# A re-ordered preamble, and the small loads moved from ScalarE's queue to SyncE's, in a fused cross-attention and rank-8 feed-forward kernel

## The chip, the cores and the metric

The kernel runs on one core of a Trainium2 chip. The metric is the device time of one execution in microseconds (us); lower is better. Five engines work side by side and meet only at semaphores: TensorE (PE in the profile: matmuls, with PEld for its weight loads), VectorE (DVE), ScalarE (ACT), GpSimd (POOL) and SyncE (SP), which computes nothing and here issues most DMA transfers. ScalarE can issue DMAs too ("ACTq" in the profile, "SPq" for SyncE's).

## The reference

All tensors are float32. x is (8, 1024, 1024): 8 batches of 1024 rows. A memory of 64 rows per batch is attended to, and then eight 1024 x 1024 matrices are applied to the same rows and summed.

```
h   = layernorm(x)
s   = h @ mem[b].T / sqrt(1024);  s = where(mask[b], s, -1e30)
x   = x + where(any(mask[b]), softmax(s) @ mem[b], 0)
h2  = layernorm(x)
x   = x + sum_r(h2 @ factors[r]) / sqrt(8) + bias        # r = 0..7
```

Because the eight products are only summed, `h2 @ factors[r]` summed over r is `h2 @ W` with W the sum of the eight matrices. The kernel forms W once, 32 MB of loads for 4 MB of weights.

## The kernel before, in words

**Tiling.** The 8192 rows are 16 groups of 512 (`g`); a group is four tiles of 128 rows (`t`), or two pairs of them (`q`). Two groups share a batch and so a memory.

**Program order is a table.** The kernel runs under a manual schedule: what a step issues to an engine stands in that engine's queue in the order of the text. `START` (L22) is a list of 259 steps that prepares the weights and the first two groups; `LOOP` then runs once per group. Every step is a small function; its arguments are numbers in the text. Each engine works through its own share of the steps strictly in that order and waits where an operand is not there yet.

**The ahead-of-loop work.** For groups 0 and 1: `load_rows g t` (L321) brings 128 rows; `row_stats g t` (VectorE, L371 and L372) takes mean and variance; `transpose_x_pe g h` (TensorE, L400, copied out by ScalarE at L401) transposes two tiles; `scores g` (L428) multiplies with the transposed memory, `scores_back g` turns it round, `softmax g` (VectorE L457 and L459, then ScalarE), `weights_back g`, `read_out g q n` (TensorE, L496) and `residual g q n` (VectorE, L504) add the attention's result to x. `norm_sums`, `norm_squares` and `normalize` are the second layernorm on ScalarE; `transpose_h_pe` transposes its result for group 0.

**The weights.** W is built in four shards `s` of 256 rows. `load_factor s r` (L704) brings a 1 MB piece of matrix r. A piece is then added in one of two ways: `add_factor s r` on VectorE, two adds of 128 x 1024 (L719; the first piece of a shard costs nothing, since its add comes with the second), or `sum_factor s r` on TensorE, four matmuls with the identity that sum into PSUM (L734). `add_sums s n` (L744) adds those PSUM sums to the weights, two VectorE adds. Shards 0 and 1 give the quarters b11 and t2 (at first b12), shards 2 and 3 give b21 and b22.

**The product.** It is a Strassen-Winograd scheme with seven products of halves instead of eight, so VectorE also forms differences of weights: t1 (L748), t2 (L750), t3 (L751) and t4 (L753). `product g q p` (L621) is one such product for a pair of tiles (128 x 512 by 512 x 512); `combine_rows` forms the sums of the rows (s1 to s4), `give g q p` (L634) adds a result to x. Products 2, 3, 4 and 5 are split once more by the same scheme into `part`, `combine_parts`, `combine_factors` (L764 to L767) and `give_part` (L685). A product that adds into the same PSUM bank as an earlier one waits until `give` has read the earlier value. `product 0 0 1` needs b11, `product 0 0 5` needs t1; `product 0 0 6` needs the finished t2, so all eight matrices of every shard.

**Buffers.** `bigs` are ten 8 KB-per-partition tiles that hold factor pieces, transposed rows, normalized rows and blocks in turn, given out first in, first out; `banks` are the eight PSUM banks, handled the same way.

**Later groups.** From group 2 on, rows are also loaded by `load_blocks g h` (L313, four DMAs of 256 KB) and transposed on VectorE by `transpose_blocks` (L385); from group 1 on, `relayout g q` (16 DMAs of 64 KB, L580) and `transpose_rows` (L589) transpose the normalized rows. `add_bias g q k` adds the bias on GpSimd (L570).

**Queues.** SyncE issues all loads and stores but these, which ScalarE issues: the mask to all partitions (L247) and twice to a small tile (L249), the memory of batch 0 (L271 and L272), and the bias (L264). Eight DMA completion semaphores (called lanes here) are shared by all DMAs, so a DMA waits until the one eight places before it has landed.

Of the kernel before, what the change touches and what calls it, by code (L numbers as in the profile page):

```python
# [30 lines left out]
add_factor 1 6; weights_back 0; scores_back 1; read_out 0 0 0; add_factor 0 2; read_out 0 1 0;  # L31
softmax 1; read_out 0 0 1; residual 0 0 0; residual 0 0 1; load_factor 1 2; load_factor 1 0;
load_factor 0 6; read_out 0 1 1; load_factor 1 5; weights_back 1; norm_sums 0 0; add_factor 1 3;
residual 0 1 1; load_factor 1 7; residual 0 1 0; add_factor 0 6; add_factor 1 7; sum_factor 1 0;
add_factor 1 2; load_factor 1 4; sum_factor 1 1; norm_squares 0 0; read_out 1 1 0;
load_factor 0 7; load_factor 0 3; read_out 1 0 1; load_factor 0 4; normalize 0 0 0;
normalize 0 0 1; norm_sums 0 1; sum_factor 1 4; residual 1 1 0; load_factor 3 7; add_factor 0 7;
transpose_h_pe 0 0 0; read_out 1 0 0; residual 1 0 0; norm_squares 0 1; load_factor 3 5;
read_out 1 1 1; residual 1 0 1; sum_factor 1 5; transpose_h_pe 0 0 1; load_factor 0 0;
residual 1 1 1; add_sums 1 1; load_factor 0 1; add_sums 1 0; add_factor 0 3; combine_rows 0 0 1;  # L40
sum_factor 3 5; add_factor 0 1; norm_sums 1 1; sum_factor 3 7; normalize 0 1 0; sum_factor 0 4;
normalize 0 1 1; add_factor 0 0; load_factor 3 3; load_factor 3 2; sum_factor 3 3; norm_sums 1 0;
combine_rows 0 0 2; add_sums 0 1; load_factor 3 4; norm_squares 1 0; load_factor 3 6;
add_factor 3 2; transpose_h_pe 0 1 0; add_sums 0 0; load_factor 3 0; load_factor 3 1;
add_factor 3 4; load_factor 2 3; load_factor 2 6; load_factor 2 1; add_factor 3 0;
add_factor 3 1; normalize 1 0 0; transpose_h_pe 0 1 1; load_bias; product 0 0 5; load_factor 2 2;
give 0 0 5; sum_factor 3 6; load_factor 2 7; add_bias 0 0 2; norm_squares 1 1; load_factor 2 4;
combine_rows 0 1 1; product 0 0 1; combine_rows 0 0 3; add_factor 2 6; product 0 1 1;
add_sums 3 1; combine_parts 0 4 1; add_sums 3 0; sum_factor 2 2; give 0 1 1; give 0 0 1;
# [5 lines left out]
part 0 4 1; combine_factors 4; product 0 0 7; give_part 0 4 1; combine_parts 0 4 4; part 0 4 5;  # L55
combine_rows 0 1 2; part 0 4 6; combine_rows 0 1 3; product 0 1 6; combine_factors 2;
give_part 0 4 6; combine_rows 0 1 4; combine_parts 0 2 1; part 0 2 1; give_part 0 4 5;
give 0 0 7; transpose_rows 1 0 0; add_bias 0 1 2; part 0 4 7; combine_parts 0 2 2;
load_blocks 2 0; part 0 4 3; transpose_blocks 2 1 0; give_part 0 4 3; transpose_rows 1 0 1;
part 0 2 5; combine_parts 0 2 3; give_part 0 2 5; give_part 0 4 7; add_bias 1 1 1; give 0 1 6;  # L60
combine_parts 0 3 1; give_part 0 2 1; product 1 0 1; transpose_blocks 2 1 1;
transpose_blocks 2 0 0; load_rows 2 2; transpose_blocks 2 0 1; load_rows 2 1; row_sums 2 0;
add_bias 0 1 1; part 0 3 1; part 0 4 4; give_part 0 3 1; normalize 1 1 1; transpose_blocks 2 1 2;
part 0 2 6; combine_parts 0 2 4; give_part 0 4 4; store 0 2; product 0 1 7; combine_rows 1 0 1;
part 0 2 3; transpose_blocks 2 0 2; load_rows 2 3; give 1 0 1; transpose_blocks 2 1 3;
row_sums 2 1; combine_parts 0 3 2; combine_parts 0 3 3; transpose_blocks 2 0 3;
combine_rows 1 0 2; row_squares 2 0; combine_factors 3; relayout 1 1; scores 2; product 1 0 6;
scores_back 2; give 0 1 7; combine_factors 5; give_part 0 2 6; part 0 3 6; part 0 2 2;
row_squares 2 1; softmax 2; give_part 0 3 6; combine_parts 0 3 4; part 0 3 5; give 0 1 5;
part 0 2 7; give_part 0 2 7; part 0 3 2; store 0 3; add_bias 0 0 1; give_part 0 3 5;  # L70
give_part 0 2 2; add_bias 0 1 0; add_bias 1 0 2; part 0 3 7;
"""

LOOP = """
# [32 lines left out]
def kernel(  # L107
# [17 lines left out]
    nc = tc.nc  # L125
    P = 128
# [53 lines left out]
    mask8 = const.tile([B, P // M, M], mask.dtype, name="mask8")  # L180
# [3 lines left out]
    bias_bc = const.tile([P, D], F32, name="bias_bc")  # L184
# [45 lines left out]
    st = {}  # L230
# [12 lines left out]
    def constants():  # L243

        room = bigs.take("mask", [P, 2, 8 * P], "mask_room")
        st["mask"] = room[:, 0, : B * M].bitcast(mask.dtype)[:, : B * M], room[:, 1, : B * M]
        nc.scalar.dma_start(st["mask"][0], mask.rearrange("b m -> (b m)").partition_broadcast(P))  # L247
        for h in range(P // M):
            nc.scalar.dma_start(mask8[:, h], mask)  # L249

    def masks():
        raw, maskf = st.pop("mask")
# [8 lines left out]
        banks.back("mask")  # L261

    def load_bias():
        nc.scalar.dma_start(bias_bc, bias.partition_broadcast(P))  # L264

    def load_memory(g: int):

        b = g // GPB
        m = work.tile([P, D], F32, tag="mem", name=f"mem_{b}")
        eng = nc.sync if g else nc.scalar  # L270
        eng.dma_start(m[:M], mem[b])  # L271
        eng.dma_start(m[M:], mem[b])  # L272
        st["mem", b] = m
# [550 lines left out]
```

## Time and profile before

| | us |
|---|---|
| median of 3 runs | 943.55 |
| lowest and highest run | 941.28 and 943.91 |
| the profiled execution | 941.54 |
| its span | 939.8 |
| TensorE busy | 916.9 (98% of the span) |
| VectorE busy | 783.4 (83%) |
| ScalarE busy | 458.9 (49%) |
| GpSimd busy | 265.2 (28%) |

Times below are counted from the start of the span. The clock granted to TensorE is 1.00 in every stretch. The DMA queues moved 167.04 MB; SyncE's queue carried 165.20 MB of it and ScalarE's 1.12 MB.

The DMA row of the profile shows how the work falls into two stages: in the first four of 40 slices (about 94 us) the queues move 313, 421, 420 and 421 GB/s, and afterwards less than half of that on average. The first stage is `START`: 32 factor pieces of 1 MB arrive, eight row tiles, one memory. From 107 us on TensorE stands still nowhere: all its idle time after that instant that the waits of TensorE name is zero. Matmul durations in the profile overlap (a 128 x 512 matmul is listed at 592 to 597 ns, while eight of them follow each other in 3.43 us, so 0.43 us each); sums below use the distance between starts.

### The profile page before, as it was taken

The page shows a single profiled execution, that of the slowest core. Times are in us where ns is not written, and L with a number is a line of the kernel's source. Part 1 is how long each engine was busy: PE and PEld are TensorE (multiplying, and loading weights), DVE is VectorE, ACT ScalarE, POOL GpSimd, SP SyncE. Part 2 cuts the span into 40 slices and gives each one's busy share as a digit, 9 for nine tenths or more (in the row PEclk, how much of TensorE's full clock was granted, in tenths as well). Part 3 has the DMA queues.
Part 4 walks back from the last instruction along what each step waited for, and adds up shares of the span by engine and source line. Part 5 has one row for each costly group of instructions (what it writes and reads, how often), then busy time and mean ns, then how long its engine had stood idle before and what let it go on. Part 6 is the DMA issues. An engine that isn't in the chain of part 4 may idle for free.

```text
span 939.8 us, 11731 instructions
## 1 busy us (share of the span) xinstructions
PE 916.9 (98%) x3637; PEld 578.2 (62%) x3637; DVE 783.4 (83%) x1619; ACT 458.9 (49%) x836; POOL 265.2 (28%) x355
## 2 busy tenths in 40 slices
PE   4899999999999999999999999999999999999998
PEld 4444456756657565666656575665756666665766
DVE  4799998969698896969698897969889797979876
ACT  4573233638464463737555373836545464745100
POOL 0202023515133231514233151513323151423221
PEclk9999999999999999999999999999999999999999
DMA  8999767476574847467484846558484856641412
GB/s 313 421 420 421 205 160 187 139 164 177 142 188 122 213 136 165 146 166 191 122 199 125 206 145 159 157 148 202 121 193 139 182 153 157 171 134 57 128 46 89
DMA packets 93565, 167.04 MB, mean 178 GB/s; under 512 B 12352, under 2 KB 71872, under 8 KB 89408
## 3 DMA queue, kind: packets, MB, share of 16 engines
q1 hardware_dynamic: 93024, 165.20, 61.9%
q10 hardware_dynamic: 480, 1.12, 0.4%
q8 instruction: 28, 0.46, 0.2%
q14 instruction: 33, 0.27, 0.1%
HBM read 101.25 MB, written 33.55 MB: 143 GB/s over the span
## 4 chain that ended last, share of the span: by engine, by line
PE 92%; DMA 6%; DVE 1%; ACT 1%; issue 0%; SPq 0%; POOL 0%; DVEq 0%
PE yu L621 34%; PE ro L496 6%; PE y5u L671 6%; PE y2u L671 6%; PE y4u L671 6%; PE y3u L671 6%; PE scT L428 6%; DMA f<-in_L_ffn_factors_dram 5%; PE y3v L671 3%; PE y5v L671 3%; PE y2v L671 3%; PE y4v L671 3%; PE sum L734 2%; PE y3z L671 1%; PE y2z L671 1%; PE y5z L671 1%
## 5 line engine op out<-in xcount | busy, mean ns | idle before, releaser
L570 POOL TENSOR_TENSOR x<-x,bias_bc 128x512 f32<-128x512 f32 x128 | 170.2, 1342 | 130.0 <-DVE x L685 51.6
L589 DVE STREAM_TRANSPOSE hT<-hb 128x1024 f32<-128x1024 f32 x60 | 72.7, 1231 | 59.7 <-DMA hb<-h 55.4
L532 ACT ACTIVATE junkz<-x 128x1024 bf16<-128x1024 f32 x64 | 67.6, 1057 | 109.0 <-DVE x L504 108.0
L621 PE MATMUL yu<-t,s 128*128 128x512 f32 x256 | 115.3, 593 | 1.9 <-DVE t L750 1.9
L621 PE MATMUL yu<-b,hT 128*128 128x512 f32 x256 | 114.9, 592 | 0.0
L621 PE MATMUL yu<-t,hT 128*128 128x512 f32 x256 | 112.6, 592 | 0.0
L563 ACT ACTIVATE h<-x,nb,rstd 128x512 f32<-128x512 f32 x128 | 96.5, 825 | 24.8 <-POOL rs L335 13.5
L504 DVE SCALAR_TENSOR_TENSOR x<-ro,rden,x 128x512 f32<-128x512 f32 x128 | 88.6, 746 | 13.2 <-PE ro L496 13.0
L634 DVE SCALAR_TENSOR_TENSOR x<-yu,x 128x512 f32<-128x512 f32 x128 | 82.8, 678 | 3.3 <-PE yu L621 3.2
L621 PEld LDWEIGHTS yu<-t,hT 128*128 128x128 f32 x256 | 48.6, 190 | 54.0 <-issue 52.6
L385 DVE STREAM_TRANSPOSE xT<-xb 128x256 f32<-128x256 f32 x224 | 81.6, 411 | 0.0
L621 PEld LDWEIGHTS yu<-t,s 128*128 128x128 f32 x256 | 48.5, 190 | 50.6 <-issue 46.3
L543 ACT ACTIVATE junky<-x,zm 128x1024 bf16<-128x1024 f32 x64 | 73.5, 1149 | 11.1 <-POOL zm L330 8.5
L621 PEld LDWEIGHTS yu<-b,hT 128*128 128x128 f32 x256 | 48.6, 190 | 48.4 <-issue 46.9
L330 POOL TENSOR_SCALAR zm<-zs 128x2 f32<-128x2 f32 x28 | 9.8, 351 | 223.9 <-ACT junkz L532 223.9
L347 ACT ACTIVATE junk<-x 128x1024 bf16<-128x1024 f32 x56 | 58.9, 1052 | 26.1 <-DMA x<-in_x_dram 25.2
L359 ACT ACTIVATE junk<-x,nmean 128x1024 bf16<-128x1024 f32 x56 | 64.3, 1148 | 7.1 <-POOL nmean L330 4.9
L496 PE MATMUL ro<-mem,eT 64*128 64x512 f32 x256 | 64.8, 615 | 0.6 <-DVE x L504 0.4
L428 PE MATMUL scT<-xT,memT 128*64 128x256 f32 x512 | 58.8, 382 | 0.0
L685 DVE SCALAR_TENSOR_TENSOR x<-y3u,x 128x256 f32<-128x256 f32 x64 | 26.7, 418 | 37.5 <-PE y3u L671 30.3
L428 PEld LDWEIGHTS scT<-xT,memT 128*64 128x64 f32 x512 | 35.3, 137 | 21.1 <-issue 4.3
L734 PE MATMUL sum<-f,ident 128*128 128x512 f32 x96 | 42.8, 597 | 2.3 <-DMA f<-in_L_ffn_factors_dram 2.1
(148 smaller groups left out, 1631.5 us busy)
## 6 DMA issues: line engine op xcount, KB each, us to landing
x<-in_x_dram SPq DMA_DIRECT2D x64, 512.0 KB, 3.5
f<-in_L_ffn_factors_dram SPq DMA_DIRECT2D x32, 1024.0 KB, 11.4
out_dram<-x SPq DMA_DIRECT2D x64, 512.0 KB, 3.1
hb<-h SPq DMA_DIRECT2D x480, 64.0 KB, 2.0
xb<-in_x_dram SPq DMA_DIRECT2D x112, 256.0 KB, 7.5
mem<-in_ctx_dram SPq DMA_DIRECT2D x14, 256.0 KB, 6.3
mem<-in_ctx_dram ACTq DMA_DIRECT2D x2, 256.0 KB, 9.4
bias_bc<-in_L_ffn_bias_dram ACTq DMA_DIRECT2D x1, 512.0 KB, 8.1
```

The lines of the kernel that those rows point to most:

```text
L385: nc.vector.transpose(xT[:, 2 * e + c].rearrange("p (t j) -> p t j", j=Q), xb.rearrange("p t (k e i c) -> p e c t k i", e=NC // 2, i=2, c= ...
L428: nc.tensor.matmul(ps[ts(h, M), : 2 * P], mT[:, c, :], st["xT", g, h][:, c, :], start=(c == 0), stop=(c == NC - 1),)
L496: nc.tensor.matmul(ps, eT[ts(h, M), q, :], m[ts(h, M), ts(n, H)], start=True, stop=True)
L504: nc.vector.scalar_tensor_tensor(xt, st.pop(("ro", g, q, n, h)), rden[:, k : k + 1], xt, ALU.mult, ALU.add)
L532: nc.scalar.activation(junk, st["x", g, 2 * h + q], AF.Copy, accum_out=s1[:, h : h + 1])
L543: nc.scalar.activation(junk, st["x", g, 2 * h + q], AF.Square, bias=nmean[:, h : h + 1], accum_out=ss[:, h : h + 1])
L563: nc.scalar.activation(to, fr, AF.Identity, bias=nb[:, h : h + 1], scale=rstd[:, h : h + 1])
L570: eng.tensor_add(xt, xt, bias_bc[:, ts(k % 2, H)])
L589: nc.vector.transpose(st["hT", g, q][:, h].rearrange("p c (t j) -> p t c j", j=Q), hb[:, h].rearrange("p t (c i) -> p t c i", i=Q),)
L621: nc.tensor.matmul(ps, lhs[:, c, :], wq[right][:, c, :], start=(first and c == 0), stop=(c == KH - 1), skip_group_check=True,)
L634: nc.vector.scalar_tensor_tensor(xt, st["y", g, q, key], ISR, xt, ALU.mult, ALU.add)
L671: nc.tensor.matmul(ps, lhs[:, c, :], right[:, c, :], start=(first and c == 0), stop=(c == 1), skip_group_check=True,)
```

## The change

It does three things.

1. `START` is replaced by another order of the same kinds of steps. It holds 259 steps as before. The rows of group 0 are loaded first, those of group 1 after factor pieces have been asked for; `scores 0` and `scores 1`, which were steps 23 and 32 (counted from 0), are steps 21 and 49. The factor pieces come in another order, shard by shard less strictly (pieces of shards 2 and 3 before the last ones of shard 1). Which pieces go to which engine changes too: `add_factor` 22 times instead of 20, `sum_factor` 10 times instead of 12.
2. The DMAs of the mask, of the memory of batch 0 and of the bias are issued by SyncE instead of ScalarE. `load_bias` was step 121 and is step 168, behind `relayout 1 0`; `scores 2`, step 235 before, is step 202.
3. Nothing in `LOOP` changes.

```diff
 START = """
-load_rows 1 0; constants; load_rows 0 0; load_rows 0 1; load_rows 0 2; load_memory 0;
-row_stats 1 0; load_rows 1 1; transpose_x_pe 0 0; row_stats 0 0; centre_memory 0; load_rows 0 3;
-transpose_x_pe 1 0; load_rows 1 2; masks; transpose_memory 0; load_factor 0 5; add_factor 0 5;
-row_stats 0 1; load_factor 1 6; transpose_x_pe 0 1; load_rows 1 3; row_stats 1 1; scores 0;
-scores_back 0; row_stats 0 2; load_factor 1 3; transpose_x_pe 1 1; row_stats 0 3;
-load_factor 0 2; softmax 0; load_factor 1 1; scores 1; row_stats 1 2; row_stats 1 3;
...
-sum_factor 2 7; load_factor 2 0; add_bias 0 0 3; add_factor 2 3; part 0 4 2; load_factor 2 5;
-combine_parts 0 4 2; add_factor 2 1; sum_factor 2 0; product 0 1 5; combine_rows 0 0 4;
-add_factor 2 4; give_part 0 4 2; combine_parts 0 4 3; load_memory 2; load_rows 2 0;
-normalize 1 0 1; relayout 1 0; add_factor 2 5; centre_memory 2; normalize 1 1 0; add_sums 2 1;
-product 0 0 6; load_blocks 2 1; add_sums 2 0; add_bias 0 1 3; give 0 0 6; transpose_memory 2;
...
+load_rows 0 0; load_rows 0 1; load_rows 0 2; constants; load_memory 0; load_rows 0 3;
+row_stats 0 0; centre_memory 0; load_rows 1 2; load_rows 1 3; row_stats 0 1; load_factor 1 5;
+load_factor 1 0; transpose_x_pe 0 0; masks; row_stats 0 2; transpose_memory 0;
+transpose_x_pe 0 1; row_stats 0 3; add_factor 1 5; load_factor 0 1; scores 0; load_rows 1 0;
+load_rows 1 1; row_stats 1 0; load_factor 0 0; add_factor 0 1; add_factor 1 0; scores_back 0;
+load_factor 0 5; softmax 0; load_factor 0 3; load_factor 0 7; transpose_x_pe 1 0;
+load_factor 0 4; load_factor 1 2; row_stats 1 1; row_stats 1 2; weights_back 0; add_factor 0 3;
+row_stats 1 3; transpose_x_pe 1 1; load_factor 0 6; load_factor 0 2; read_out 0 1 1;
+read_out 0 1 0; read_out 0 0 1; residual 0 1 0; read_out 0 0 0; scores 1; residual 0 0 0;
...
+load_factor 2 3; normalize 1 0 0; add_sums 3 1; combine_rows 0 0 2; add_sums 3 0;
+combine_rows 0 0 3; load_factor 2 5; sum_factor 2 1; normalize 1 1 0; sum_factor 2 7;
+add_factor 2 4; normalize 1 0 1; load_memory 2; product 0 1 5; give 0 1 1; sum_factor 2 5;
+add_factor 2 3; combine_rows 0 0 4; add_sums 2 1; add_sums 2 0; product 0 0 5;
+combine_parts 0 4 1; product 0 0 6; combine_factors 4; combine_rows 0 1 2; load_blocks 2 0;
+part 0 4 2; part 0 4 1; give 0 0 6; part 0 4 5; combine_parts 0 4 2; combine_rows 0 1 3;
+normalize 1 1 1; transpose_blocks 2 0 0; give_part 0 4 2; combine_parts 0 4 3; relayout 1 0;
+load_bias; combine_rows 0 1 4; centre_memory 2; transpose_memory 2; combine_parts 0 4 4;
+product 0 1 6; combine_parts 0 2 1; transpose_blocks 2 0 1; load_rows 2 2; give_part 0 4 1;
+part 0 2 1; load_blocks 2 1; product 0 0 7; part 0 4 6; give_part 0 4 5; combine_factors 2;
...
@@ constants
-        nc.scalar.dma_start(st["mask"][0], mask.rearrange("b m -> (b m)").partition_broadcast(P))
+        nc.sync.dma_start(st["mask"][0], mask.rearrange("b m -> (b m)").partition_broadcast(P))
         for h in range(P // M):
-            nc.scalar.dma_start(mask8[:, h], mask)
+            nc.sync.dma_start(mask8[:, h], mask)
@@ load_bias
-        nc.scalar.dma_start(bias_bc, bias.partition_broadcast(P))
+        nc.sync.dma_start(bias_bc, bias.partition_broadcast(P))
@@ load_memory
-        eng = nc.sync if g else nc.scalar
+        eng = nc.sync
```

More of the change, by code (lines that the diff above doesn't have):

```diff
@@ L31 @@
[L31 to L48, printed above, removed]
@@ L49 @@
-add_sums 3 1; combine_parts 0 4 1; add_sums 3 0; sum_factor 2 2; give 0 1 1; give 0 0 1;
-sum_factor 2 7; load_factor 2 0; add_bias 0 0 3; add_factor 2 3; part 0 4 2; load_factor 2 5;
-combine_parts 0 4 2; add_factor 2 1; sum_factor 2 0; product 0 1 5; combine_rows 0 0 4;
-add_factor 2 4; give_part 0 4 2; combine_parts 0 4 3; load_memory 2; load_rows 2 0;
-normalize 1 0 1; relayout 1 0; add_factor 2 5; centre_memory 2; normalize 1 1 0; add_sums 2 1;
-product 0 0 6; load_blocks 2 1; add_sums 2 0; add_bias 0 1 3; give 0 0 6; transpose_memory 2;
@@ L55 @@
[L55 to L71, printed above, removed]
+load_rows 0 0; load_rows 0 1; load_rows 0 2; constants; load_memory 0; load_rows 0 3;
@@ new lines @@
+row_stats 1 3; transpose_x_pe 1 1; load_factor 0 6; load_factor 0 2; read_out 0 1 1;
+read_out 0 1 0; read_out 0 0 1; residual 0 1 0; read_out 0 0 0; scores 1; residual 0 0 0;
+load_factor 3 2; residual 0 0 1; scores_back 1; add_factor 0 4; softmax 1; load_factor 3 6;
+load_factor 2 6; add_factor 0 6; residual 0 1 1; sum_factor 0 0; weights_back 1; norm_sums 0 0;
+load_factor 2 2; load_factor 1 6; read_out 1 0 1; norm_squares 0 0; add_factor 0 7;
+add_factor 1 2; load_factor 1 1; sum_factor 0 5; residual 1 0 1; load_factor 1 4; read_out 1 0 0;
@@ new lines @@
+add_factor 3 2; norm_sums 0 1; sum_factor 0 2; normalize 0 0 0; add_factor 3 6; add_sums 0 1;
+load_factor 2 0; add_factor 2 6; residual 1 0 0; load_factor 1 7; read_out 1 1 1;
+norm_squares 0 1; add_factor 2 2; add_sums 0 0; load_factor 3 4; sum_factor 1 6; norm_sums 1 0;
+normalize 0 0 1; add_factor 1 1; load_factor 1 3; residual 1 1 1; load_factor 3 7;
+read_out 1 1 0; normalize 0 1 0; residual 1 1 0; normalize 0 1 1; load_factor 3 1;
+add_factor 2 0; sum_factor 1 4; transpose_h_pe 0 0 0; add_factor 3 4; sum_factor 1 7;
@@ new lines @@
+load_factor 3 3; add_factor 1 3; add_sums 1 1; add_sums 1 0; add_factor 3 1;
+transpose_h_pe 0 1 0; transpose_h_pe 0 1 1; load_factor 3 0; load_factor 3 5;
+transpose_h_pe 0 0 1; add_factor 3 3; product 0 1 1; add_factor 3 0; norm_squares 1 0;
+load_factor 2 1; combine_rows 0 0 1; add_factor 3 7; combine_rows 0 1 1; product 0 0 1;
+sum_factor 3 5; norm_sums 1 1; load_factor 2 7; load_factor 2 4; give 0 0 1; norm_squares 1 1;
+load_factor 2 3; normalize 1 0 0; add_sums 3 1; combine_rows 0 0 2; add_sums 3 0;
@@ new lines @@
+load_bias; combine_rows 0 1 4; centre_memory 2; transpose_memory 2; combine_parts 0 4 4;
+product 0 1 6; combine_parts 0 2 1; transpose_blocks 2 0 1; load_rows 2 2; give_part 0 4 1;
+part 0 2 1; load_blocks 2 1; product 0 0 7; part 0 4 6; give_part 0 4 5; combine_factors 2;
+give 0 0 5; give_part 0 4 6; part 0 4 3; transpose_blocks 2 1 0; transpose_blocks 2 1 1;
+transpose_blocks 2 0 2; give_part 0 2 1; part 0 2 5; transpose_blocks 2 0 3;
+transpose_blocks 2 1 2; transpose_blocks 2 1 3; give_part 0 4 3; part 0 4 7; add_bias 0 0 2;
@@ new lines @@
+combine_parts 0 2 2; add_bias 0 0 3; give_part 0 4 7; load_rows 2 0; scores 2; add_bias 0 1 2;
+part 0 2 6; add_bias 0 0 1; transpose_rows 1 0 0; give 0 1 5; add_bias 0 1 1; give 0 0 7;
+part 0 4 4; transpose_rows 1 0 1; give_part 0 2 5; give_part 0 2 6; combine_parts 0 2 3;
+combine_parts 0 2 4; give 0 1 6; give_part 0 4 4; combine_parts 0 3 1; part 0 3 1;
+combine_rows 1 0 1; combine_parts 0 3 2; load_rows 2 1; store 0 2; load_rows 2 3; product 1 0 1;
+part 0 2 2; row_sums 2 0; give 1 0 1; part 0 2 3; part 0 2 7; give_part 0 3 1; row_squares 2 0;
@@ L72 @@
+combine_parts 0 3 3; combine_factors 3; combine_rows 1 0 2; combine_factors 5; product 0 1 7;
+part 0 3 5; scores_back 2; part 0 3 6; give_part 0 3 6; relayout 1 1; row_sums 2 1;
+product 1 0 6; row_squares 2 1; part 0 3 7; combine_parts 0 3 4; give 0 1 7; add_bias 1 0 2;
+softmax 2; give_part 0 2 7; give_part 0 3 5; give_part 0 2 2; add_bias 0 1 3; store 0 3;
+add_bias 0 1 0; add_bias 1 1 1; part 0 3 2;
 """
```

## The prediction

> **What bounds the kernel now.** I read the busy shares first, then the waits of TensorE over the whole span, then the order of time of TensorE and VectorE up to 130 us. TensorE is busy 98% of the span; its named waits come to 18 us, and all lie ahead of 107.5 us:
>
> ```profile
> PE tp L400 <- DMA x<-in_x_dram: 11.1, 2, 7.9
> PE sum L734 <- DMA f<-in_L_ffn_factors_dram: 2.1, 3, 1.0
> PE yu L621 <- DVE t L750: 1.9, 1, 1.9
> ```
>
> So the time is the instant at which `product 0 0 6` starts, plus TensorE's work behind it, plus what TensorE waits behind it (nothing now). That instant is set by this chain, TensorE first, then VectorE:
>
> ```profile
> 101.99 3.60 PE L621 MATMUL yv<-t,s 128*128 128x512 f32 x8
> 107.47 3.70 PE L621 MATMUL yu<-t,s 128*128 128x512 f32 x8 [1.89 <-DVE t L750]
> ...
> 102.40 2.36 DVE L719 TENSOR_TENSOR b<-b,f 128x1024 f32<-128x1024 f32 x2 [1.03 <-DMA f<-in_L_ffn_factors_dram]
> 104.87 1.29 DVE L744 TENSOR_TENSOR b<-sum,b 128x512 f32<-128x512 f32 x2
> 106.19 1.22 DVE L750 TENSOR_TENSOR t<-b,t 128x1024 f32<-128x1024 f32 x1
> ```
>
> The last factor piece lands at 102.4, VectorE adds it, adds the PSUM sums and forms t2, and TensorE starts at 107.47. The stage is limited by three things at once, as the windows show (columns: stretch, its length, busy us and instructions of TensorE, its loads, VectorE, ScalarE, GpSimd; clock; DMA share; GB/s):
>
> ```profile
> 20.00:45.00 25.00, 23.15 (x135) 12.97 (x135) 19.62 (x35) 14.41 (x39) 5.12 (x7) 1.00 1.01 420
> 45.00:70.00 25.00, 23.33 (x71) 10.46 (x67) 23.25 (x27) 18.77 (x33) 1.08 (x3) 1.00 1.01 420
> 70.00:95.00 25.00, 24.46 (x69) 11.46 (x68) 24.22 (x28) 8.68 (x15) 6.50 (x8) 1.00 1.01 421
> ```
>
> DMA is full, TensorE 93 to 98% busy, VectorE 78, 93 and 97%. A change gains only if it relieves all three.
>
> **Part 1: the loads.** TensorE waits for its seventh factor piece until 37.29 and VectorE for its 23rd until 77.00: 39.71 / 16 = 2.48 us a piece. The queues never starve, so in the new order the k-th piece (with all eight row tiles ahead of it) lands at 37.29 + 2.48 (k - 7) - g, g being what the start gains. What is g? The first 12 us move little: 208 GB/s on average up to 10 us against 420 later. SyncE's fourth load waits there 4.6 us for the mask, its first factor 2.8 us for the memory, since the eight lanes are shared:
>
> ```profile
> SPq L321 <- DMA mask_room<-in_mask_BxS_bk_dram: 4.6, 1, 4.6
> SPq L704 <- DMA mem<-in_ctx_dram: 2.8, 1, 2.8
> ```
>
> The upper end is g = 3: some 1.5 us lost between 8 and 12 us at 209 to 270 GB/s, and as much ahead of 6 us. The Trainium skill (DMA: Bandwidth & Descriptors, "Issuing engines are not separate DMA queues") speaks against a gain: DMAs of different engines run on the same 16 DMA engines and interleave, and a second issuing engine saves only issue time. By it g = 0, and SyncE pays ScalarE's issues (0.41 + 0.88 + 0.63 + 0.71 = 2.6 us), which is hidden, since its next load waits for the first to land anyway. The nearest row takes the rule's side in part: memory landed 9.4 us after issue on ScalarE's queue at the start, and 8.6 us on SyncE's at 95 us. It is slow by itself. But the mask no longer stands in the lanes ahead of the row tiles, and the bias (0.5 MB, 1.2 us) no longer ahead of the last pieces. I take g = 1. The last (32nd) piece then lands at 37.29 + 62.0 - 1 = 98.3, 4.1 us earlier than now; its four identity matmuls (1.7) end at 100.0. TensorE's early start is worth nothing: with rows 0 0 and 0 1 first it begins near 6 us instead of 11.6, but `transpose_x_pe 1 0` then waits for tiles that lie behind three factor pieces. `scores 1` ends near 40 us instead of 31. TensorE catches up later, for it has two `sum_factor` fewer: 8 x 0.43 = 3.4 us, and these are off the path, because VectorE is what comes last.
>
> **Part 2: VectorE up to t2.** Its queue is in order, and `row_stats 1 0` now stands ahead of every add. Tile 1 0 lands one tile (1.25) and one piece ahead of the fourth piece: 37.29 - 3 x 2.48 - 1 - 2.48 - 1.25 = 25.1 us. Until then VectorE idles some 10 us. From there to the end of t2 it has, by distances between starts in the trace:
>
> - 4 `row_stats` x 1.40 = 5.6 (two of these were done by 23 us before)
> - 18 pairs of adds x 2.27 = 40.9 (before 16; two more cost 4.5)
> - 8 `residual` x 1.31 = 10.5; 7 pairs of `add_sums` x 1.27 = 8.9
> - 6 weight differences = 7.3; 5 `combine_rows` x 0.61 = 3.1; 2 gives = 1.2; softmax 1.4
>
> Together 78.8. The same list for before gives 75.0 where the trace has 76.2 (84.5 us from 22.96 to 107.45 less 8.3 idle), so I add 1.7%: 80.1. One wait goes in: the pair that needs the sixth piece (33.8) is reached at 32.4, 1.4 us. Later pieces are there: the 22nd lands at 73.5 and is needed at 73.6. t2 is ready at 25.1 + 80.1 + 1.5 = **106.7**, 0.8 earlier than now, though loading ended 4 us earlier. In this list the differences t2 and t4 are priced quiet; one t2 difference took 1.89 us before while GpSimd added the bias (85.0 to 86.3), 1.22 otherwise. The bias adds now all come later, where they may cost as much: five of them at up to 0.67 each, 0 to 3.4 us, mostly beside slack; I take 0.
>
> **Part 3: behind `product 0 0 6`.** TensorE's work there grows by `part 0 4 2`, which was ahead of it: 0.86. Then VectorE's queue against TensorE's, both counted from 106.7: VectorE forms t3, t4, `combine_factors 4` and s2 by 7.3, TensorE reaches t4 0.3 too early and s2 another 0.4 too early. `scores 2` now comes 18 us behind `product 0 0 6` (before 27.7). Its chunks wait for `transpose_blocks 2 1`, which VectorE reaches at 17.0 and ends at 21.5; TensorE stands 0.5. Sum of waits 1.2. Afterwards TensorE is behind VectorE again: `part 0 2 6` at 22.6 needs s2 at 22.2, `product 1 0 1` at 25.2 needs rows transposed at 23.7.
>
> SyncE in this stretch: `relayout 1 0` waits for the buffer of `add_factor 2 4` (100.7), issues 16 DMAs at 0.64 (their distance from 108.7 on) to 0.91 (the mean of 97.92 to 112.51), then bias 0.36, rows 0.45 and four blocks at 0.5, and the blocks land 7.2 later: 121 to 125. Needed at 106.7 + 17.0 = 123.7. I take 121, as the slow issues before were those beside the last factor. GpSimd waits for the bias but nothing on TensorE's path waits for it soon.
>
> **Sum:** -0.8 + 0.86 + 1.2 = +1.3 us on the profiled execution's 941.54 (span 939.8): 942.8. That execution is 2.0 below the median of three (943.55); I place the forecast half way between the two bases, 943.8, rounded to **944**. About 0.3% (2.8 us) is what a measurement of this kernel can tell from no change.
>
> **Rivals.**
> 1. *Loading sets it, faster.* If VectorE's tile comes with g = 3 (23.1) and the ledger needs no 1.7%, t2 would follow loading: 96.3 + 1.7 + 3.4 (`product 0 0 5`) = 101.4 at best, and VectorE at 103.4. Product 0 0 6 is then 4.1 early: 941.5 - 4.1 + 0.9 + 0.7 = 939.0. For it: the first 12 us are visibly slow. Against: two adds more on an engine that was 97% busy, and slow memory loads.
> 2. *The blocks land late, slower.* `load_blocks 2 1` stands behind 16 relayout DMAs and the bias, and `scores 2` was moved forward. It decides once they land after 123.7. At 0.91 an issue they are issued by 118, and as slow as before (two sets of blocks took 114 to 124 us) they land at 128: 4.3 us of VectorE in order and so of TensorE: 942.8 + 4.3 = 947.1, 948 on the half-way basis. For it: the order of SyncE's queue. Against: in the quiet stretch issues were 0.64 apart.
> 3. *Nothing.* The stage is bound by three resources, and the two adds just fill what the loads gain: that is nearly the main case.
>
> **Chances.** Main case 0.55, own range 940.5 to 948.5; rival 1 0.22, 939 to 940; rival 2 0.23, 947 to 951. From these: faster by over 0.3% (below 940.7) 0.21, slower by over 0.3% (above 946.4) 0.39 (all but 0.03 of rival 2, and 0.19 of the main case, because such a ledger leaves waits out more easily than in), within 0.40. Range 939.5 to 949.5.
>
> **What would show it.** In the profile after: last factor piece landing near 98 (wait of TensorE or VectorE for f); VectorE idle from about 14 to 25 us waiting for x; TensorE waiting several us for VectorE ahead of `product 0 0 1` (b11) and again ahead of `product 0 0 6`, which starts near 106.7; short waits behind it at L671 and L428. A start of `product 0 0 6` near 103 speaks for rival 1, a wait of `transpose_blocks` on xb near 124 for rival 2. The forecast is wrong if row tile 1 0 lands far from 25, or if LOOP's first group shows waits on TensorE.

## The result and the profile after

The changed kernel takes 944.68 us (median of 11 runs, 943.72 to 947.61), the kernel before 941.54 (median of 11 runs beside them, 941.0 to 945.68). The ratio is 1.0029, with a 95% interval of 1.0015 to 1.0043: slower by 0.3%. The profiled execution of the changed kernel took 944.41 us (span 942.6), that of before 941.54 (span 939.8): 2.9 us apart.

These are TensorE's longest waits in the changed kernel (us in total, times, longest). All lie ahead of `product 0 0 6`:

```profile
PE tp L401 <- DMA x<-in_x_dram: 7.8, 4, 4.2
PE tp L401 <- DVE t L745: 2.8, 1, 2.8
PE sum L735 <- DMA f<-in_L_ffn_factors_dram: 2.4, 3, 1.4
PE memTp L302 <- ACT memc L287: 2.4, 1, 2.4
```

The row of before that had VectorE's t2 as the last releaser (`PE yu L621 <- DVE t L750: 1.9`) has no counterpart. TensorE no longer waits for t2. The order of time of TensorE shows what it did instead (start, length, line, tiles, count; in brackets an idle time ahead of it and its releaser):

```profile
77.35 1.49 PE L401 MATMUL tp<-ident,h 128*128 128x128 f32 x8 [2.78 <-DVE t L745]
78.63 8.59 PE L622 MATMUL yu<-b,hT 128*128 128x512 f32 x16
87.06 10.46 PE L735 MATMUL sum<-f,ident 128*128 128x512 f32 x24
97.36 3.60 PE L622 MATMUL yv<-t,s 128*128 128x512 f32 x8
101.56 3.70 PE L735 MATMUL sum<-f,ident 128*128 128x512 f32 x8 [0.61 <-DMA f<-in_L_ffn_factors_dram]
105.10 3.60 PE L622 MATMUL yv<-t,s 128*128 128x512 f32 x8
108.54 3.60 PE L622 MATMUL yu<-t,s 128*128 128x512 f32 x8
```

From 77.35 on it works with one gap of 0.61 us. The row at 108.54 is `product 0 0 6`. Count backwards from it: one product, one sum, one product, three sums. Each of them is four matmuls, which stand in the trace as eight records (x8), 0.43 us apart. That makes six blocks of 3.43 us (the distance of the last two starts), 20.6 us behind 87.06, and the gap at the last piece. VectorE over the same time:

```profile
24.09 1.29 DVE L372 BATCH_NORM_STATS2 stx<-x 128x6 f32<-128x512 f32 x2 [9.77 <-DMA x<-in_x_dram]
...
104.26 0.68 DVE L745 TENSOR_TENSOR b<-sum,b 128x512 f32<-128x512 f32 x1
105.30 0.69 DVE L745 TENSOR_TENSOR b<-sum,b 128x512 f32<-128x512 f32 x1 [0.36 <-PE sum L735]
106.03 1.22 DVE L751 TENSOR_TENSOR t<-b,t 128x1024 f32<-128x1024 f32 x1
```

t2 is ready at 107.25 (106.03 + 1.22), and TensorE comes for it only 1.29 us later. The three long windows (columns as in the prediction):

```profile
20.00:45.00 25.00, 19.96 (x103) 12.84 (x100) 18.21 (x30) 8.44 (x27) 1.21 (x2) 0.80 1.01 419
45.00:70.00 25.00, 22.45 (x62) 8.95 (x61) 24.88 (x30) 19.83 (x36) 3.56 (x6) 1.00 1.01 421
70.00:95.00 25.00, 22.22 (x66) 11.08 (x65) 23.73 (x26) 16.55 (x27) 5.62 (x6) 0.93 1.01 421
```

DMA is as full as before. TensorE is busy 80 to 90% instead of 93 to 98%, and its granted clock, 1.00 all through before, is 0.80 and 0.93. Windows of 5 us show where:

```profile
25.00:30.00 5.00, 3.94 (x16) 3.25 (x16) 4.83 (x10) 1.46 (x8) 0.00 (x0) 0.50 1.01 421
30.00:35.00 5.00, 4.75 (x23) 4.03 (x25) 3.47 (x6) 4.54 (x11) 0.00 (x0) 0.62 1.01 418
...
75.00:80.00 5.00, 2.65 (x10) 1.76 (x11) 4.86 (x7) 2.06 (x4) 0.00 (x0) 0.82 1.01 421
80.00:85.00 5.00, 5.00 (x11) 2.09 (x10) 5.00 (x6) 4.84 (x10) 2.81 (x3) 0.84 1.02 423
```

**Where the 2.9 us come from.** `product 0 0 6` starts 1.07 us later (108.54 against 107.47). Behind it TensorE has `part 0 4 2` more (0.86), its starts fall behind by 0.61 more up to 152 us and by 0.27 more in the loop (both are differences of starts; its waits name no cause for them): TensorE's last y3v group starts at 936.89 instead of 934.08, 2.81 us later.

The 1.07 us are a balance of larger sums. Up to `product 0 0 6`, TensorE of before is busy 89.29 us of 107.47, TensorE of after 88.55 of 108.54. The changed kernel has two sums and `part 0 4 2` less in that stretch, 2 x 3.43 + 0.86 = 7.7 us. But it is busy only 0.74 us less, so the rest of its work took some 7.0 us longer. The lowered clock accounts for about that: (1 - clock) x 5 us, summed over the windows below 1.00 (0.86, 0.50, 0.62, 0.82, 0.84), is 6.8 us. And it is not busy for 20.0 us instead of 18.2. So -7.7 + 7.0 + 1.8 = +1.1. This account says what TensorE's time consisted of, not which wait ended last; that is what the runs below are for.

### The profile page after: what moved, and what is told of

Same layout as the page of the kernel before. It is cut to its first block, busy times and chain, and to the rows that moved or that the text cites. A ratio compares the mean times of both kernels' runs of the same rounds, so it can differ in the third digit from the quotient of the medians.

```text
span 942.6 us, 11708 instructions
## 1 busy us (share of the span) xinstructions
PE 917.8 (97%) x3621; PEld 579.5 (61%) x3621; DVE 787.3 (84%) x1623; ACT 459.4 (49%) x836; POOL 267.6 (28%) x355
## 4 chain that ended last, share of the span: by engine, by line
PE 88%; DMA 7%; DVE 3%; SPq 1%; issue 0%; ACT 0%; DVEq 0%; ACTq 0%
PE yu L622 33%; PE ro L497 6%; PE y5u L672 6%; PE y2u L672 6%; PE y3u L672 6%; PE y4u L672 5%; PE scT L429 5%; DMA f<-in_L_ffn_factors_dram 3%; PE y3v L672 3%; PE y5v L672 3%; PE y2v L672 3%; PE y4v L672 3%; DMA xb<-in_x_dram 2%; PE sum L735 2%; PE y3z L672 1%; PE y2z L672 1%
## 5 line engine op out<-in xcount | busy, mean ns | idle before, releaser
L438 ACT ACTIVATE scTs<-scT,maskT 128x256 f32<-128x256 f32 x16 | 7.6, 473 | 93.9 <-PE scT L429 93.9
```

## The experiments

Theories: **A**, the new order makes the loss, and the queue does not; **B**, the queue makes part of it. **C**, TensorE comes last ahead of `product 0 0 6`; **D**, VectorE does, as the prediction had it. The runs were timed beside the kernel before, whose median was 941.57, 941.53 or 941.46 us (23, 11 and 27 executions). A ratio is to that kernel, with its 95% interval.

### The order alone, the queue alone

The two parts of the change, one each:

```diff
 START = (the new order)
-        nc.sync.dma_start(bias_bc, bias.partition_broadcast(P))
+        nc.scalar.dma_start(bias_bc, bias.partition_broadcast(P))
```

(likewise mask and memory of batch 0), and

```diff
-START = (the new order)
+START = (the order of before)
         nc.sync.dma_start(bias_bc, bias.partition_broadcast(P))
```

> The new order with mask, memory and bias on ScalarE's queue as before. Theory A (the order makes the loss: two adds more on VectorE, b11 finished later, so TensorE starts its products late): 944 to 946 us, ratio to before 1.002 to 1.004. Theory B (the queue makes the loss, by putting slow small loads ahead of the row tiles): 941 to 942.5, ratio within 0.001 of 1.

> The old order with mask, memory and bias on SyncE's queue. Theory A: 940.5 to 942 us, ratio 0.999 to 1.0005; row tiles at the start land up to 3 us earlier, but factor pieces only about 0.7 us earlier. Theory B: 944 us or more, ratio 1.002 or more.

Measured: the order alone 945.12 us (944.31 to 946.12), ratio 1.0033 [1.0022, 1.0044]. The queue alone 942.57 (940.60 to 951.82, 14 runs), ratio 1.0020 [1.0001, 1.0039]. The order alone brings the whole loss: A. The queue alone gains nothing that the time shows; its median lies between the two forecasts, and its interval, 0.01 to 0.39%, leaves room for a small loss too. In its profiled execution (941.42 us) `product 0 0 6` starts 0.86 us earlier than before, and the time is no different; but six of its 14 executions lie above 944 us, of before 3 of 23. In the order-alone run, TensorE's order of time has the last piece later than in the changed kernel:

```profile
97.66 3.60 PE L622 MATMUL yv<-t,s 128*128 128x512 f32 x8
102.69 3.70 PE L735 MATMUL sum<-f,ident 128*128 128x512 f32 x8 [1.43 <-DMA f<-in_L_ffn_factors_dram]
106.23 3.60 PE L622 MATMUL yv<-t,s 128*128 128x512 f32 x8
109.66 3.60 PE L622 MATMUL yu<-t,s 128*128 128x512 f32 x8
```

So under the new order the move to SyncE's queue goes with 1.1 us at `product 0 0 6` in the profiled executions; the medians, 0.44 us apart, do not tell the two kernels apart.

### One sum more, one sum less

A factor piece moved from VectorE to TensorE, and another from TensorE to VectorE, each from the changed kernel:

```diff
-add_factor 3 0
+sum_factor 3 0
```

```diff
-sum_factor 2 7
+add_factor 2 7
```

> The changed kernel with add_factor 3 0 turned into sum_factor 3 0: one pair of adds (2.27 us) less on VectorE, one sum (eight matmul records, 3.44 us) more on TensorE, late in the stage. Theory C (as measured: TensorE works without a gap from 78 us to product 0 0 6 and is last): about 3.4 us slower than the changed kernel, 947.5 to 948.5. Theory D (as predicted: VectorE is last and TensorE has 3.5 us of slack there): 1 to 2 us faster than the changed kernel, 942.5 to 943.5.

> The changed kernel with one factor piece of quarter 2 (piece 2 7) moved the other way than in the one-more-sum run: sum_factor to add_factor, 3.43 us less on TensorE, some 2.3 us more on VectorE. By the prediction's own picture (VectorE comes last ahead of product 0 0 6) t2 is 2.3 us later and so is the time, about 947. By theory C (TensorE comes last, and VectorE was 1.3 us ahead of it: t2 ready at 107.25, product 0 0 6 at 108.54) the first 1.3 us cost nothing and VectorE takes over as the last: product 0 0 6 near 109.5 (+1.0), the time +0.5 to +1.2 on the changed kernel, 945.2 to 945.9. So the split is balanced within a piece, and no choice of it brings the loss back.

One sum more: 947.10 us, ratio 1.0057 [1.0042, 1.0072], 2.4 us above the changed kernel. From 83.53 on TensorE runs without a gap, and it starts `product 0 0 6` at 111.10:

```profile
83.53 3.70 PE L735 MATMUL sum<-f,ident 128*128 128x512 f32 x8 [0.65 <-DMA f<-in_L_ffn_factors_dram]
87.06 3.60 PE L622 MATMUL yu<-b,hT 128*128 128x512 f32 x8
90.50 10.46 PE L735 MATMUL sum<-f,ident 128*128 128x512 f32 x24
...
111.10 3.17 PE L622 MATMUL yu<-t,s 128*128 128x512 f32 x7
```

The added sum is the row at 83.53. VectorE lost a pair of adds and still the start moved 2.56 us later: C, and D falls. It is 2.56 and not 3.43 because the 0.88 us that the changed kernel loses at the last piece are gone (and so the time, forecast as 947.5 or more, is 947.10).

One sum less: 945.85 us, ratio 1.0043 [1.0031, 1.0055]. `product 0 0 6` starts at 109.11, as forecast, and now it does wait for t2:

```profile
109.11 3.70 PE L622 MATMUL yu<-t,s 128*128 128x512 f32 x8 [0.67 <-DVE t L751]
```

Each engine is the last one as soon as it is given one piece more. The split of the changed kernel is balanced to within one piece, and neither of these two neighbours is better.

### The quarter that TensorE waits for, earlier

Pieces 1 7 and 1 3 are loaded ahead of 2 0 and 3 4, and added ahead of them, so that shard 1 is complete sooner and TensorE does not wait at 77 us (the cut shows the adding):

```diff
-add_factor 2 0; sum_factor 1 4; transpose_h_pe 0 0 0; add_factor 3 4; sum_factor 1 7;
-load_factor 3 3; add_factor 1 3; add_sums 1 1; add_sums 1 0; add_factor 3 1;
+add_factor 1 3; sum_factor 1 4; transpose_h_pe 0 0 0; sum_factor 1 7;
+load_factor 3 3; add_sums 1 1; add_sums 1 0; add_factor 2 0; add_factor 3 4; add_factor 3 1;
```

> The changed kernel with the pieces of shard 1 loaded and added ahead of pieces 2 0 and 3 4, so that b11 is complete some 4 us earlier; same steps, same counts. Theory C1 (what holds product 0 0 6 is the late b11 and the slow clock behind TensorE's wait there): products with b11 start near 74 instead of 78.6 at clock 1.00 (eight matmul records in 3.43 instead of 4.2 us), product 0 0 6 starts 1 us or more earlier, 943.5 or less. Theory C2 (the last factor piece, landing at 101.6, and TensorE's 6.9 us behind it hold it just as well): same earlier products, but product 0 0 6 near 108.4 and the time within 0.5 us of 944.7.

Measured: 945.32 us (944.73 to 946.29), ratio 1.0037 [1.0024, 1.0051]. TensorE's order of time:

```profile
75.01 7.03 PE L622 MATMUL yu<-b,hT 128*128 128x512 f32 x16
86.98 12.82 PE L735 MATMUL sum<-f,ident 128*128 128x512 f32 x24 [4.93 <-DMA f<-in_L_ffn_factors_dram]
99.63 3.60 PE L622 MATMUL yv<-t,s 128*128 128x512 f32 x8
```

The wait at 77 us is gone, the two products start 3.6 us earlier and run at full clock. Nothing comes of it: TensorE then waits 4.93 us for the 27th factor piece, starts its sums within 0.1 us of the time in the changed kernel, and runs them 2.4 us longer, at a clock of 0.50 just behind the wait. The idle time had only moved, as the second theory said; that the slow clock would move with it was not foreseen, and `product 0 0 6` starts at 109.93 instead of the 108.4 of that theory.

### The memory later, and the waiting filled

The memory load, which stands right behind the last factor piece in SyncE's queue, moved behind the first blocks; in the second run also the 16 transposes ahead of the wait at 77 us issued twice into the same place:

```diff
-add_factor 2 4; normalize 1 0 1; load_memory 2; product 0 1 5
+add_factor 2 4; normalize 1 0 1; product 0 1 5
...
-combine_rows 0 1 2; load_blocks 2 0;
+combine_rows 0 1 2; load_blocks 2 0; load_memory 2;
```

```diff
+                    for _ in range(twice):
-                    nc.tensor.transpose(ps[:, ts(c * n + t, P)], cols, ident)
+                        nc.tensor.transpose(ps[:, ts(c * n + t, P)], cols, ident)
```

> The changed kernel with load_memory 2 moved behind load_blocks 2 0, so that no 64-row memory load follows straight on the last factor piece in Sync's queue. Theory E1 (the memory load shares the DMA engines with the last piece and stretches its tail from some 98 to 101.5 us): the last piece lands by 99.5, the 0.61 us in which TensorE waits for it are gone, product 0 0 6 starts near 107.9 instead of 108.5, and the time is some 0.6 us below the changed kernel's 944.7. Rival E2 (the tail has another cause: the pieces' own period): the last piece still lands at 101 to 101.7, TensorE still waits 0.5 us or more, and the time is that of the changed kernel, 944.2 to 945.2.

> The run with the memory load later, and besides the 16 transposes of h for the second quarter, which end 2.8 us before TensorE gets its next bank, are each issued twice into the same place (same result), so that about 1.9 of these 2.8 us are filled with work that adds nothing. Theory K1 (the waiting just before lowers the granted clock in 75 to 85 us, and that costs the two b11 products 8.4 - 6.9 = 1.5 us): the clock there goes from 0.82/0.84 to above 0.93, the products take 7.0 to 7.4 us, product 0 0 6 starts about 1 us earlier than in the run with the memory load later alone, and the time is about 1 us lower. Rival K2 (the clock follows something that lies further back, such as the 20 to 35 us stretch, or the waiting only moves): the clock in 75 to 85 stays below 0.88 and the products at 8 us or more, or TensorE waits the gain away at the last piece; the time stays within 0.4 us of the run with the memory load later alone.

The memory later: 945.68 us, ratio 1.0041 [1.0028, 1.0054], no gain; both forecasts of the time (944.1, and 944.2 to 945.2) missed. The last piece's packets still ended at 100.3 us (100.0 in the changed kernel), so the memory as such is not the cause of the late end; the blocks had taken its place. TensorE does not wait for that piece, but it also comes for it later, at 101.77: its clock in 75 to 85 us was 0.65 and 0.67 this time. Behind `product 0 0 6` (108.68) it loses some 0.9 us more than the changed kernel up to the first y3v group (143.52 against 142.46).

With the waiting filled: 944.42 us, ratio 1.0030 [1.0018, 1.0042]. The clock is 1.00 in both windows, and the products take 7.11 us instead of 8.59. The order of time of TensorE:

```profile
73.28 3.66 PE L402 MATMUL tp<-ident,h 128*128 128x128 f32 x32
77.95 1.25 PE L402 MATMUL tp<-ident,h 128*128 128x128 f32 x8 [1.02 <-DVE t L746]
79.24 7.11 PE L623 MATMUL yu<-b,hT 128*128 128x512 f32 x16
87.22 10.70 PE L736 MATMUL sum<-f,ident 128*128 128x512 f32 x24 [0.87 <-DMA f<-in_L_ffn_factors_dram]
```

The 1.5 us are waited away at the 27th piece (0.87), and `product 0 0 6` starts at 109.20. The clock is as the first theory had it, and the time ahead of `product 0 0 6` as its rival had it: at full clock too TensorE cannot start these sums before the piece is there. The time is 1.3 us below the run with the memory later alone, with overlapping intervals; the number is the first theory's, but the path is not, since `product 0 0 6` starts 0.52 us later. What is gained in the two profiled executions lies behind it: from there to the last y3v group it is 827.97 us against 829.65. Why was not found.

### Nothing but small packets behind the last piece

Blocks and memory both behind `relayout 1 0`, with the steps that need them later:

```diff
-add_factor 2 4; normalize 1 0 1; load_memory 2; product 0 1 5
+add_factor 2 4; normalize 1 0 1; product 0 1 5
...
-combine_rows 0 1 2; load_blocks 2 0;
+combine_rows 0 1 2;
...
-give_part 0 4 2; combine_parts 0 4 3; relayout 1 0;
+give_part 0 4 2; combine_parts 0 4 3; relayout 1 0; load_blocks 2 0; load_memory 2;
```

> The changed kernel with both loads that follow straight on the last factor piece (blocks 2 0 and memory 2) moved behind relayout 1 0, which Sync issues only after the relayout's rows are ready, so that nothing but the relayout's small packets can share the DMA engines with the last piece; the first block transposes, and memory 2's centring and transposes, stand later too. Theory E3 (whatever load is queued right behind the last piece stretches its tail, memory or blocks alike): the last piece's packets end by 98.0, 2.5 to 3.4 us after the one before it, instead of 100.0 to 101; TensorE's wait for it is gone, and product 0 0 6 starts at 107.6 to 108.1 instead of 108.5. Rival E4 (the last piece is slow by itself, since its last packets sit on few DMA engines): its packets still end at 99.5 or later. The time is not what this run is for: the blocks come later, so it may lie anywhere from 944 to 948.

The last piece's packets ended at 98.9 us, neither by 98.0 nor after 99.5. That is 4.3 us behind the piece before it, where the other runs of this order have 4.7 (one sum more) to 6.9 (order alone), and the relayout's own packets were beside them from 96 us on. But before has 4.3 too, with the memory behind its last piece, and the one-sum-more run has 4.7 with both loads there. The packets that ran beside the last piece say more: in before and with the queue alone they were the memory's (97 and 113 of 4 KB) and none of the blocks', and the tail is 4.3 and 4.2 us; with 26, 98 and 199 packets of the blocks beside it (one sum more, one less, the changed kernel) it is 4.7, 5.1 and 5.6, and with 236 to 754 in the other four 5.7 to 6.9. So the longer tails go with the blocks and not with the memory; but a longer tail also meets more packets, so which brings which is not shown. TensorE, at full clock in 75 to 85 us, waits 0.86 us for the 27th piece, starts its sums 0.68 us earlier than in the changed kernel, does not wait for the last piece, and starts `product 0 0 6` at 107.22, 1.3 us earlier than in the changed kernel and 0.25 earlier than before:

```profile
96.92 3.60 PE L622 MATMUL yv<-t,s 128*128 128x512 f32 x8
100.35 3.60 PE L735 MATMUL sum<-f,ident 128*128 128x512 f32 x8
103.79 3.60 PE L622 MATMUL yv<-t,s 128*128 128x512 f32 x8
107.22 3.60 PE L622 MATMUL yu<-t,s 128*128 128x512 f32 x8
...
128.74 2.37 PE L429 MATMUL scT<-xT,memT 128*64 128x256 f32 x18 [2.50 <-DVE xT L386]
```

The last row is most of the price: the blocks come late, VectorE waits 2.82 us for a load ahead of their transposes, TensorE 2.50 for VectorE (3.6 us in all its waits for VectorE), and the time is 948.06 us (ratio 1.0065 [1.0045, 1.0086]). This is the prediction's second rival, made by hand.

### The order of before on SyncE's queue, improved

Two attempts at a kernel that beats both: bias, memory and rows of group 2 all behind the end of the factors, and then only bias and rows.

```diff
-load_bias; product 0 0 5; load_factor 2 2;
+product 0 0 5; load_factor 2 2;
...
-combine_parts 0 4 3; load_memory 2; load_rows 2 0; normalize 1 0 1; relayout 1 0;
+combine_parts 0 4 3; load_memory 2; normalize 1 0 1; relayout 1 0; load_bias; load_rows 2 0;
```

> The order of before on Sync's queue, with what was queued ahead of the end of the factors moved behind it: load_bias behind load_factor 2 5, load_memory 2 and load_rows 2 0 behind load_blocks 2 0, the two row tiles' bias behind that, and memory 2's centring and transposes just ahead of scores 2. Theory A+E1 (before's order keeps TensorE at full clock and its share of the sums leaves VectorE last; the loads ahead of the last pieces cost some tenths): the last factor piece lands near 98 to 99, product 0 0 6 starts at 105.9 to 106.6 (106.61 in the run that changes the queue alone, 107.47 before), and the time is 939.5 to 941, below both kernels. Rival (what is won ahead of product 0 0 6 is lost behind it, since the later memory load makes scores 2 late, or the later bias makes the rows late): 941.5 to 943.

> The order of before on Sync's queue with only the bias and rows 2 0 moved, behind relayout 1 0 in Sync's queue, and the two row tiles' bias on GpSimd that would wait for it moved behind the third; memory 2 and the blocks stay where they were. Theory (the bias ahead of the last five pieces costs them 0.6 to 0.9 us on Sync's queue): the pieces from the 27th on land 0.6 to 0.9 us earlier than in the run that changes the queue alone, product 0 0 6 starts at 105.7 to 106.3 (106.61 there, 107.47 before), and if nothing behind takes it back the time is 940.0 to 941.5. Rival (VectorE has work without a gap there, so that product 0 0 6 stays at 106.4 to 106.8): 941 to 942.6, no different from before.

Both miss. The edit shown is the second (two of the bias adds on GpSimd move behind the third with it); the first also has `load_memory 2` and `load_rows 2 0` behind `load_blocks 2 0`, the bias behind the last piece, and memory 2's centring and transposes just ahead of `scores 2`. The first took 967.80 us (ratio 1.0258 [1.0222, 1.0295]). Memory 2's centring was reached by ScalarE at 155.8 us, and TensorE waited for it:

```profile
PE memTp L302 <- ACT memc L289: 16.0, 2, 15.7
```

The second has 22 executions in two groups, 12 at 942.2 to 944.2 and 10 at 949.9 to 955.1 us (median 944.07, ratio 1.0056 [1.0033, 1.0080]). Even the lower group is not faster than before. The profiled execution (949.92) belongs to the upper one, so whether the pieces came earlier in the lower group was not seen. What it shows is one small instruction of GpSimd that took 6.31 us:

```profile
42.84 6.31 POOL L338 TENSOR_SCALAR rstd<-zq 128x2 f32<-128x2 f32 x1 [11.25 <-ACT junky L544]
...
42.21 1.21 DVE L720 TENSOR_TENSOR b<-b,f 128x1024 f32<-128x1024 f32 x1
...
47.89 1.21 DVE L720 TENSOR_TENSOR t<-t,f 128x1024 f32<-128x1024 f32 x1
```

VectorE adds six times without a gap from 42.21 to 49.10, and GpSimd's instruction ends at 49.15. In the first attempt it takes 6.32 us and ends 0.05 us behind six such adds as well. In the queue-alone run it takes 1.77 us: there VectorE waits 0.68 us for a factor piece behind its second add, and GpSimd's instruction ends 0.05 us behind that add. So in these two kernels the very wait of VectorE that let GpSimd through was gone. Behind it ScalarE stood idle for 7.49 us, TensorE waited for ScalarE and gave a buffer back late, and the packets of the 19th factor piece ended at 70.9 us instead of 64.5; `product 0 0 6` started at 111.98, 5.4 us later than in the queue-alone run. Whether the lower group, and the slow executions of the queue-alone run, differ in just this was not seen. No version beat the kernel before.

### What the runs say together

TensorE's time from the start of its last three sums in a row (24 records) to `product 0 0 6`, in us:

| kernel | sums start | waits behind, and a clock below 1 | `product 0 0 6` | distance |
|---|---|---|---|---|
| changed | 87.06 | 0.61 for the last piece | 108.54 | 21.48 |
| order alone | 87.35 | 1.43 for the last piece | 109.66 | 22.31 |
| one sum more | 90.50 | none | 111.10 | 20.60 |
| quarter earlier | 86.98 | 2.36, slow clock | 109.93 | 22.95 |
| memory later | 88.04 | none | 108.68 | 20.64 |
| waiting filled | 87.22 | 0.89 for the last piece | 109.20 | 21.98 |
| blocks later | 86.38 | none | 107.22 | 20.84 |

The distance is 20.6 us, six times 3.43, plus what the third column names, to within half a microsecond. The sums start when the 27th factor piece has landed (86.4 to 87.2 us in the four runs that wait for it) and the two products ahead of them are done. In the changed kernel the products end just then, at 87.06, without a wait. So the loads leave little to be won ahead of the sums: 0.68 us in the run with the later blocks, the earliest of the four. What is won beyond that is waited away. The run with one sum less is the exception that fits: there VectorE is the last. Behind `product 0 0 6` it is 828.35 us to the last y3v group in the changed kernel, and 826.61 before.

## Why the prediction was right or wrong

The time, 944.68, and its side were as forecast (944, range 939.5 to 949.5). That the number fits is luck. The forecast step was +1.3 us on the profiled execution, which turned out +2.9 (medians: +3.1), and the half-way base added 1.0 that the measured median of before (941.54) does not have. Term by term, the -0.8 for the start of `product 0 0 6` became +1.07, the 0.86 for `part 0 4 2` held, and the 1.2 of waits behind it became 0.88.

- **The loads.** The period was right: the packets of the 7th to the 31st piece end 34.55 to 94.44 us, 2.50 us a piece. By the ends of the packets g was 0.6 (the 7th piece ends at 34.55 instead of 35.14); the prediction took 1, and by the rule of the Trainium skill that it names (DMA: Bandwidth & Descriptors, "Issuing engines are not separate DMA queues") it would be 0. With the order alone it is 0.25, with the queue alone 0.64, so the move between queues brings the pieces some 0.3 to 0.6 us forward, which the rule does not have; but no time was shorter for it, which is the rule's side. The last piece was to be there at 98.3. Its packets ended at 100.0, 5.6 us behind those of the piece before it instead of 2.5, and TensorE started on it at 101.56, 3.3 us later than the sum had it.
- **The failed step** is the sentence that the last piece's four identity matmuls take 1.7 us, and that two `sum_factor` fewer are "8 x 0.43 = 3.4 us, and these are off the path, because VectorE is what comes last". The 0.43 us are the distance of two records, and a matmul is two records here (also where the time section above says matmuls): a `sum_factor` takes 3.43 us, two of them 6.9. The size was halved, and with it TensorE's side of the sum was only the last piece plus 1.7 plus 3.4, 103.4. Its own queue ahead of that was never added up. Done with before's numbers it would have been: 27th piece at 37.29 + 20 x 2.48 - 1 = 85.9, plus 20.6, so 106.5. That is a tie with VectorE's 106.7, not an engine off the path. It became 108.54: the sums started 1.2 us later than that, and 0.88 were lost at the late last piece. The runs with one sum more and one less show the tie: 2.56 us later on the one side, 0.57 on the other.
- **VectorE up to t2** was nearly right: tile 1 0 at 24.09 (25.1), the wait for the next pair 1.49 us (1.4), t2 ready at 107.25 (106.7). Between the two it took 1.6 us longer than forecast: it waited 3.4 us for factor pieces where 1.5 were taken and 0.4 for TensorE's last sum, and its work was some 0.7 shorter. It was not what came last. TensorE does not wait for VectorE at `product 0 0 6`, where the prediction expected several us; its one long wait for VectorE, 2.8 us at 77.35, is near `product 0 0 1` as expected, but for a PSUM bank that `add_sums 1` frees.
- **Behind `product 0 0 6`**: 0.86 for `part 0 4 2` as predicted; 0.61 and 0.27 lost elsewhere instead of 1.2, and none of it named as a wait at the places predicted. VectorE waited 0.37 us for the blocks at 124.99: the second rival was close, and did not decide. The run with the later blocks shows what it would have cost.
- **Rivals 1 and 3.** Loading did set the time in part, through the 27th piece, but with 20.6 us of TensorE behind it there was little to gain from it. "Nothing" (a ratio of 1) is outside the interval of the ratio, 1.0015 to 1.0043.
- **Not foreseen**: the clock. It cost TensorE some 6.8 us of its own time. About 5 of these lie between 20 and 35 us, and no run of this order was at full clock there; behind them TensorE waits for factor pieces at 59.27 (1.44 us) and 69.12 (0.40). The 1.7 us at 78 to 82 were given back in the run with the waiting filled, and were waited away at the 27th piece.

## What to carry to other kernels

Where two engines and the loads meet at one instruction, add up all three queues to that instruction, each with the number of records a step really has in the trace; the engine called off the path is the one whose sum was left out. Idle time ahead of a load that fixes the rest is worth little: ask for the last such load, and count what is behind it. A load that stands behind the last needed one can be moved away only as far as its own reader can wait.

## What the runs showed of the hardware

- **The clock after a wait.** The same wait of 2.8 us at 77 us was followed by a granted clock of 0.82 and 0.84 in the changed kernel, and by 1.00 in the runs with one sum less and with the blocks later; behind a wait of 4.93 us it was 0.50. The clock records of the traces know only full and half rate, and their half-rate stretches ahead of the loop last 3.41, 6.83 or 10.24 us (in the first attempt above, 17.07 later on): one, two, three (five) times 3.41. Cut into steps of 3.41 us in line with these changes, the two cases come apart (stretch, its length, TensorE busy, clock; the changed kernel, then the later blocks):

```profile
74.80:78.21 3.41, 0.86 (x6) 1.00 1.01 423
78.22:81.63 3.41, 3.41 (x8) 0.50 1.02 423
...
72.34:75.75 3.41, 2.00 (x17) 1.00 1.01 423
75.75:79.16 3.41, 2.00 (x10) 1.00 1.01 420
79.17:82.58 3.41, 3.41 (x9) 1.00 1.02 423
```

  In the first the wait falls into one step, in the second it is shared by two. In the twelve traces, from the first recorded change of the clock on, each of the 22 full-rate steps with 1.85 us or more of idle TensorE was followed by half rate, and each of the 3182 with 1.79 us or less by full rate. The Trainium skill (TensorE: Matmul & The Clock Gate, Part 1) has the two rates and a free-running window of about 3.4 us, which agrees with these records; it puts the limit at a gap of more than about 3.4 us, where 2.8 us were enough here.
- **The last load's tail.** A packet of 8 KB took 0.31 us through the whole of the loading, and 0.53 to 0.77 us among the last dozen of the last piece in the changed kernel, where packets of 4 KB (memory) and 1 KB (blocks) ran beside it. The last piece took 5.6 us behind its predecessor there, 5.7 with the memory moved, 4.3 with only the relayout's packets behind, but also 4.3 in the kernel before and 4.7 with one sum more, so the size of the tail is not explained.
- **GpSimd beside VectorE.** GpSimd's instruction on two columns (`rstd`) took 0.19 us in 18 of the 48 times that it stands in the first 110 us of the twelve traces, and 0.23 to 6.32 us in the other 30. Each of these 30 ended 0.05 us behind the end of a VectorE instruction with both operands in SBUF (adds of pieces, sums of rows, differences of weights). So it goes with VectorE's work on SBUF that it is held up; sometimes it came through between two adds that followed each other without a gap (0.70 us at 81.96 in the changed kernel), and in two kernels only behind six (6.31 and 6.32 us).
